# A state-space mixer on one core: SiLU halves joined, and the last quarter's input products moved to ScalarE

## The chip, the cores and the metric

The kernel runs on one core of a Trainium2 chip. The metric is device time in microseconds (us) for the whole program, which computes four layers in one launch. The engines are named as in the profile: PE (TensorE, with PEld for its weight loads), DVE (VectorE), ACT (ScalarE), POOL (GpSimd) and SP (SyncE).

## The reference, cut to what matters

The change lies in layer 0, in the state-space mixer that follows graph attention. Per batch there are 128 nodes, 32 time steps, 256 inner channels and 16 states:

```python
xz = xt @ in_proj
xc, z = xz[..., :D_INNER], xz[..., D_INNER:]
...
xc = silu(xconv)                      # causal convolution over 4 steps
dbc = xc @ x_proj
dt = softplus(dbc[..., :DT_RANK] @ dt_w + dt_b)
Bm, Cm = ...
dA = exp(dt[..., None] * A)
dBx = (dt * xc)[..., None] * Bm[:, :, None, :]
def step(hprev, inp):
    hnew = dA_t * hprev + dBx_t
    y_t = einsum('bds,bs->bd', hnew, C_t)
...
y = (ys + Dp * xc) * silu(z)
return y @ out_w + out_b
```

So each step multiplies the state by a decay, adds an input `u * B` with `u = dt * xc`, and reads the state out with `C`.

## The kernel before, in words

All of layer 0 works on the four batches one after the other. For each, `gat` computes attention, and `mamba` the state-space mixer. The state `S` lies in SBUF as 128 nodes by 16 states by 256 channels.

In `mamba` the 32 steps are cut into 8 blocks of four steps. Per block there is preparation: `mamba_block` makes the convolution (`conv`, four products per half of the channels, L889), its SiLU (`xsilu`, L896), the projections, `dt` and `u`, and the columns `B` and `C` (the tile `BC`); `mamba_gates` makes the gates (`gatep`, L852, and `zsilu`, L859). Both SiLUs work on two halves of 128x512. The first block's `mamba_block` is planned inside the attention stage, all others one block ahead inside `mamba`.

Each step works in four quarters `q` of four states each. For a quarter:

- `decay` (POOL, L667) multiplies `dt` with the rates, into `e`, a tile with three buffers
- `expo` (ACT, L673) takes the exponential into `pa`, a PSUM tile with two buffers
- `mul` (DVE, L687) multiplies `pa` by the state
- `plus` (DVE, L695) adds the input. It issues four instructions, one for each state, each of which computes `u * B + pa`, with `B` as a scale per partition. In the first step of a batch there is nothing to decay, and `plus` only makes the product (L697)
- `diag_pool` (POOL, L684, first two quarters) or `diag` (ACT, L679, last two) makes diagonal matrices of `C`
- `read` (PE, L710) multiplies them with the state and sums over the states, in the PSUM tile `yp`

After the four quarters, `fetch` (ACT, L718) copies the sum out into `y` (two buffers), `turn` (PE, L723 and L728) transposes it into a PSUM bank, and `gate` (DVE, L736) multiplies it by the SiLU of the gates. A block ends with a projection (PE, L773 to L779), a copy (ACT, L785), and a normalization on DVE, POOL and ACT.

The banks of the PSUM tag `pm`, of which there are two, are shared by `turn`, the convolution, the gates and every projection.

The order of the instructions is not written by hand. Each piece of work is a part with an engine, an estimated cost, the parts it comes after, and the buffers that it takes and frees (`hold`). The class `Parts` simulates the engines and picks, part by part, the one that can start first; among those of the same engine that can start within a short patience it takes the one of lowest rank. The rank is the step number times `pace`, plus an offset for the kind of part from the table `RANKS`. The order so found on PE, DVE, ACT and POOL is then kept in the program. Parts whose function differs in its table (`exp`, `ln`, `silu`) make ACT load a table; the load stands in the profile as ACT_TABLE_LOAD at the line of the instruction that needs it.

Of the kernel before, what the change touches and what calls it, by code (L numbers as in the profile page):

```python
# [12 lines left out]
F32 = mybir.dt.float32  # L13
# [110 lines left out]
class Parts:  # L124
# [12 lines left out]
    def hold(self, name, limit):  # L137
        self.limits[name] = limit
        return {"name": name, "free": []}
# [48 lines left out]
class Kernel:  # L188
# [393 lines left out]
    def mamba_weights(self, c, k):  # L582
# [43 lines left out]
        return (inp, xp, dtw, ow, cb, DD, I2, ob4, ntg, ntb, Ar, Wm), built  # L626

    RANKS = dict(
        back=-267, bc=-139.5, bct=18.5, conv=139.5, dabs=-39.5, dbc=10, decay=155.5, dexp=-267, diag=215.5,
        diagp=-284, dln=-315.5, dplus=-240, dsub=-168.5, dtproj=-353, expo=-4, fetch=-214, gate=-583,  # L630
        gatep=361.5, mul=112.5, norm=506.5, ofetch=-562.5, one=-558, plus=-359, power=155.5, project=146,
        read=547.5, relu=-197, shift=-23, stats=284.5, sums=33.5, turn=-293, umul=-243.5, x=667, xproj=-666,
        xsilu=235, xturn=-318, zsilu=203,
    )

    def mamba(self, b, h1, S, blk, gw, mw, m0, w0, m, w, pa, py, pm):
# [6 lines left out]
        inp, xp, dtw, ow, cb, DD, I2, ob4, ntg, ntb, Ar, Wm = mw  # L643
        PE, DVE, ACT, POOL = "PE", "DVE", "ACT", "POOL"
        plan = Parts(window=300, patience=0.15)
        hold, pace = plan.hold, 25.0

        def add(kind, at, *args, **kwargs):
            plan.rank = at * pace + self.RANKS[kind]
            return plan.add(*args, **kwargs)  # L650
# [6 lines left out]
        def step(t, g, before):  # L657

            k, i = divmod(t, 4)
            cs, h, v, parts = slice(i * P, i * P + P), g["h"], {}, {}  # L660

            def node(name):
                return g[name][:, i // 2, i % 2 * 256 : i % 2 * 256 + 256]

            def decay(q):
                v["e", q] = w.tile([P, 4, 256], F32, tag="e", name="e", bufs=3)
                nc.gpsimd.tensor_tensor(  # L667
                    v["e", q], node("dt").unsqueeze(1).to_broadcast([P, 4, 256]), Ar[:, 4 * q : 4 * q + 4, :], ALU.mult
                )

            def expo(q):
                v["a", q] = pa.tile([P, 4, 256], F32, tag="pa", name="pa")
                nc.scalar.activation(v["a", q], v.pop(("e", q)), AF.Exp, scale=-1.0)  # L673

            def diag(q):
                v["D", q] = w.tile([P, 4, 64], F32, tag="D", name="D", bufs=4)
                for r in range(4):
                    s = 16 + 4 * q + r
                    nc.scalar.activation(v["D", q][:, r, :], I2, AF.Copy, scale=g["BC"][:, i, s : s + 1])  # L679

            def diag_pool(q):
                v["D", q] = w.tile([P, 4, 64], F32, tag="Dp", name="Dp", bufs=4)
                C = g["BC"][:, i, 16 + 4 * q : 20 + 4 * q].unsqueeze(2).to_broadcast([P, 4, 64])
                nc.gpsimd.tensor_tensor(v["D", q], I2.unsqueeze(1).to_broadcast([P, 4, 64]), C, ALU.mult)  # L684

            def mul(q):
                nc.vector.tensor_tensor(v["a", q], v["a", q], S[:, 4 * q : 4 * q + 4, :], ALU.mult)  # L687

            def plus(q):
                a = v.pop(("a", q), None)  # L690
                for r in range(4):
                    s = 4 * q + r
                    Bt = g["BC"][:, i, s : s + 1]
                    if t:
                        nc.vector.scalar_tensor_tensor(S[:, s, :], node("u"), Bt, a[:, r, :], ALU.mult, ALU.add)  # L695
                    else:
                        nc.vector.tensor_scalar(S[:, s, :], node("u"), Bt, None, ALU.mult)  # L697

            def read(q):
                if q == 0:
                    v["y"] = py.tile([P, 2, 512], F32, tag="yp", name="yp")
                D = v.pop(("D", q))
                for r in range(4):
                    s = 4 * q + r
                    for n in range(2):
                        o = 64 * ((n + s) % 2)
                        ns = slice(64 * n, 64 * n + 64)
                        nc.tensor.matmul(  # L710
                            v["y"][o : o + 64, n, :256], D[ns, r, :], S[ns, s, :], start=(s < 2), stop=(s >= 14),
                            skip_group_check=True,
                        )

            def fetch():
                y = v.pop("y")
                v["y"] = w.tile([P, 2, 256], F32, tag="y", name="y")
                nc.scalar.copy(v["y"], y[:, :, :256])  # L718

            def turn():  # L720
                v["p"] = bank()
                for j in range(2):
                    nc.tensor.matmul(  # L723
                        v["p"][:, j * P : (j + 1) * P], DD[:, j, :], g["xc"][:, j, cs], start=True, stop=False
                    )
                    for n in range(2):
                        o = j * P + 64 * n
                        nc.tensor.matmul(  # L728
                            v["p"][:, o : o + 64], v["y"][:, n, j * P : (j + 1) * P], I2, start=False, stop=(n == 1)
                        )  # L730

            def gate():
                if i == 0:
                    g["yg"] = m.tile([P, 2, 4, P], F32, tag="yg", name="yg")
                p = v.pop("p")[:, :256].rearrange("p (j n) -> p j n", j=2)
                nc.vector.tensor_tensor(g["yg"][:, :, i, :], p, g["sz"][:, :, cs], ALU.mult)  # L736

            hy, hv = hold("y", 1), hold("yv", 2)
            last = []
            for q in range(4):  # L740
                p = None
                hD = hold("Dp" if q < 2 else "D", 4)
                if t:
                    he, ha = hold("e", 3), hold("pa", 2)
                    p = add("decay", t + q / 4, POOL, 2.36, lambda q=q: decay(q), [g["dt ready"]], [he], [h["dt"]])
                    p = add("expo", t + q / 4, ACT, 1.03, lambda q=q: expo(q), [p], [ha], [he], "exp")
                    p = add("mul", t + q / 4, DVE, 1.23, lambda q=q: mul(q), [p, before["plus", q]])
                if q < 2:
                    d = add("diagp", t + q / 4, POOL, 0.7, lambda q=q: diag_pool(q), [g["BC ready"]], [hD])
                else:  # L750
                    d = add("diag", t + q / 4, ACT, 1.0, lambda q=q: diag(q), [g["BC ready"]], [hD])
                p = parts["plus", q] = add(
                    "plus", t + q / 4, DVE, 1.8, lambda q=q: plus(q),
                    [p, g["u ready"][i // 2], before and before["read", q]],
                    free=[ha, h["u"]] if t else [h["u"]],
                )
                last = [parts.setdefault(("read", q), add(
                    "read", t + q / 4, PE, 1.0, lambda q=q: read(q), [p, d, *last], [] if q else [hy], [hD]
                ))]
            p = add("fetch", t + 1, ACT, 0.6, fetch, last, [hv], [hy])  # L760
            hp = hold("pm", 2)
            p = add("turn", t + 1, PE, 1.5, turn, [p], [hp] if i else [h["yg"], hp], [hv, h["xc"]])
            p = add("gate", t + 1, DVE, 0.45, gate, [p, *g["sz ready"]], (), [hp, h["sz"], h["BC"]])
            g.setdefault("gates", []).append(p)
            return parts
# [78 lines left out]
    def mamba_gates(self, g, k, add, hold, h1, mw, w, pm):  # L844
# [11 lines left out]
        def zsilu(j):  # L856
            if j == 0:
                g["sz"] = w.tile([P, 2, 512], F32, tag="sz", name="sz")
            nc.scalar.activation(g["sz"][:, j, :], g.pop(("z", j)), AF.Silu)  # L859

        zs, first = [], None
        for j in range(2):
            hp = hold("pm", 2)
            first = c = add("gatep", 4 * k, PE, 0.97, lambda j=j: gatep(j), [first], [hp] if j else [h["sz"], hp])
            zs.append(add("zsilu", 4 * k, ACT, 0.6, lambda j=j: zsilu(j), [c, *zs], (), [hp], "silu"))
        g["sz ready"] = zs

    def mamba_block(self, k, add, hold, h1, mw, m, w, pm, after=()):

# [98 lines left out]
            nc.vector.tensor_copy(g["BC"].rearrange("p a b -> p (a b)"), g.pop("bc")[:, :128])  # L968


        xs, first = [], None
        for j in range(2):
            hp = hold("pm", 2)
            first = c = add("conv", 4 * k, PE, 1.95, lambda j=j: conv(j, 0), [first, *after], [hp] if j else [h["xc"], hp])
            c = add("conv", 4 * k, PE, 1.95, lambda j=j: conv(j, 2), [c])
            xs.append(add("xsilu", 4 * k, ACT, 0.7, lambda j=j: xsilu(j), [c, *xs], (), [hp], "silu"))
        hp, hb, h1_ = hold("pm", 2), hold("dbc", 1), hold("u1", 1)
        c = add("xproj", 4 * k, PE, 1.95, xproj, xs, [hb, hp])
        c = add("dbc", 4 * k, ACT, 0.65, dbc, [c], (), [hp])
# [2035 lines left out]
```

## Time and profile before

| what | us |
|---|---|
| median of three runs | 3962.16 (3951.46 to 3969.95) |
| profiled execution, own time | 3967.12 |
| span of the profiled execution | 3965.3 |
| DVE busy in the span | 3090.5 (78%) |
| PE busy | 3227.2 (81%) |
| ACT busy | 2609.6 (66%) |
| POOL busy | 2400.4 (61%) |
| from first to last decay, four batches | 415.9, 415.6, 411.7, 415.6 |

The shares are means over the whole program. The four stretches in which decays run (1659 us together) are what the change touches, besides the first block's parts in the attention stages between them; layers 1 to 3, from about 2400 us on, have none of its code. The lines of the profile give, for a group of instructions, the line of the kernel, engine, operation, tiles written and read, shapes and count, and then busy time, the mean duration of one in ns, and the idle time of the engine ahead of them with what ended it. Groups whose instructions overlap have a busy time below count times duration.

### The profile page before, as it was taken

How to read it: one execution, taken by the hardware profiler on the slowest of the kernel's cores; microseconds unless marked ns; L12 is line 12 of the kernel's file. 1: busy time of each engine (PE TensorE's matmuls, PEld its weight loads, DVE VectorE, ACT ScalarE, POOL GpSimd, SP SyncE). 2: the span in 40 equal slices, each digit the busy share in tenths (PEclk: the TensorE clock that was granted, in tenths of full speed). 3: DMA queues.
4: the chain of work that ended last, by engine and by line, in shares of the span. 5: the costliest groups of instructions: out<-in, count | busy, mean ns of one | idle time of the engine just before them, and what ended most of it. 6: DMA issues, size and time to landing. Idle time of an engine off the chain costs nothing. (4 is left out here: it accounts for less than half of the span.)

```text
span 3965.3 us, 64167 instructions
## 1 busy us (share of the span) xinstructions
PE 3227.2 (81%) x23297; PEld 2075.9 (52%) x23297; DVE 3090.5 (78%) x7595; ACT 2609.6 (66%) x5093; POOL 2400.4 (61%) x1786
## 2 busy tenths in 40 slices
PE   6888887888888888878888869787847787988877
PEld 3445544444544454544444548655535663587655
DVE  6799997799997799997899975668757866286952
ACT  5799875798864798865899853334544556166763
POOL 2599883699873699973799860233444443066940
PEclk8999889999888999998999885888769998998999
DMA  3000000000000000000000000000020000600003
GB/s 122 1 1 1 1 1 1 1 1 1 1 1 1 1 1 1 1 1 1 1 1 1 1 17 2 1 1 1 1 87 8 1 1 1 256 7 1 1 1 86
DMA packets 51548, 61.34 MB, mean 15 GB/s; under 512 B 5743, under 2 KB 31036, under 8 KB 51100
## 3 DMA queue, kind: packets, MB, share of 16 engines
q1 hardware_dynamic: 36636, 42.12, 3.1%
q10 hardware_dynamic: 14592, 15.08, 1.1%
q8 instruction: 187, 3.06, 0.3%
q14 instruction: 133, 1.09, 0.1%
HBM read 48.79 MB, written 8.39 MB: 14 GB/s over the span
## 5 line engine op out<-in xcount | busy, mean ns | idle before, releaser
L667 POOL TENSOR_TENSOR e<-dt,Ar 128x1024 f32<-128x1024 f32 x496 | 1160.9, 2362 | 103.4 <-ACT pa L673 101.0
L695 DVE SCALAR_TENSOR_TENSOR S<-u,BC,pa 128x256 f32<-128x256 f32 x1984 | 820.8, 476 | 28.4 <-PE yp L710 0.5
L687 DVE TENSOR_TENSOR pa<-pa,S 128x1024 f32<-128x1024 f32 x496 | 607.3, 1224 | 49.3 <-ACT pa L673 49.0
L673 ACT ACTIVATE pa<-e 128x1024 f32<-128x1024 f32 x496 | 504.8, 1023 | 126.8 <-DVE S L695 114.4
L710 PE MATMUL yp<-S,D 64*64 64x256 f32 x4096 | 378.4, 414 | 101.7 <-DVE S L695 87.3
L710 PE MATMUL yp<-S,Dp 64*64 64x256 f32 x4096 | 342.9, 452 | 51.2 <-DVE S L695 38.4
L710 PEld LDWEIGHTS yp<-S,D 64*64 64x64 f32 x4096 | 186.4, 140 | 264.4 <-DVE S L695 153.8
L465 POOL TENSOR_TENSOR e<-e,den 128x512 f32<-128x512 f32 x128 | 132.2, 1043 | 257.2 <-DVE den L461 193.2
L710 PEld LDWEIGHTS yp<-S,Dp 64*64 64x64 f32 x4096 | 175.7, 153 | 203.5 <-issue 118.1
L679 ACT ACTIVATE D<-I,BC 128x64 f32<-128x64 f32 x1024 | 260.7, 334 | 0.6 <-PE yp L710 0.6
L889 PE MATMUL pm<-h,Wm 128*128 128x512 f32 x512 | 240.1, 604 | 1.2 <-ACT h L525 1.2
L728 PE MATMUL pm<-I,y 128*128 128x64 f32 x1024 | 165.1, 289 | 89.7 <-ACT y L718 89.7
L453 ACT ACTIVATE e<-sc,mn 128x128 f32<-128x128 f32 x512 | 143.9, 391 | 98.1 <-DVE mn L448 96.6
L728 PEld LDWEIGHTS pm<-I,y 128*128 128x128 f32 x1024 | 152.4, 214 | 101.9 <-ACT y L718 101.9
L673 ACT ACT_TABLE_LOAD x144 | 184.8, 1283 | 19.4 <-DVE S L695 17.2
L684 POOL TENSOR_TENSOR Dp<-I,BC 128x256 f32<-128x256 f32 x256 | 164.4, 660 | 20.1 <-PE yp L710 10.4
L251 POOL TENSOR_TENSOR rs<-rs,mhalf 128x4 f32<-128x4 f32 (+1 forms) x33 | 38.6, 1171 | 220.0 <-DVE rs L250 181.7
L448 DVE TENSOR_REDUCE mn<-sc 128x4 f32<-128x512 f32 x128 | 83.4, 685 | 87.8 <-PE sc L440 55.9
L889 PEld LDWEIGHTS pm<-h,Wm 128*128 128x128 f32 x512 | 90.9, 191 | 92.3 <-issue 90.2
L723 PE MATMUL pm<-xc,DD 128*128 128x128 f32 x512 | 127.8, 334 | 5.3 <-ACT sz L859 4.6
L723 PEld LDWEIGHTS pm<-xc,DD 128*128 128x128 f32 x512 | 87.6, 210 | 64.9 <-issue 38.0
L2607 ACT ACTIVATE xn<-X,xnb,xrs 128x128 f32<-128x128 f32 x192 | 80.7, 488 | 42.6 <-DMA lnw<-in_L_attn_ln_w_dram 30.3
(587 smaller groups left out, 8025.7 us busy)
## 6 DMA issues: line engine op xcount, KB each, us to landing
w<-in_L_ffn_weight_dram SPq DMA_DIRECT2D x22, 1024.0 KB
w<-in_L_ffn_weight_dram ACTq DMA_DIRECT2D x10, 1024.0 KB
out_dram<-o ACTq DMA_DIRECT2D x16, 256.0 KB
out_dram<-o SPq DMA_DIRECT2D x16, 256.0 KB
X<-in_x_dram SPq DMA_DIRECT2D x4, 512.0 KB
A<-in_L_conv_A_log_dram SPq DMA_DIRECT2D x1, 2048.0 KB
cw<-in_L_conv_conv_w_dram SPq DMA_DIRECT2D x1, 512.0 KB
sh<-in_sh_dram SPq DMA_DIRECT2D x1, 512.0 KB
```

What stands on the lines that cost most here:

```text
L453: nc.scalar.activation(e[:, i, :], v["sc"][:, h, i * P : (i + 1) * P], AF.Exp, scale=-1.0, bias=v["mn"][:, 4 * h + i : 4 * h + i + 1],)
L465: nc.gpsimd.tensor_tensor(v["e", h], v["e", h], den, ALU.mult)
L667: nc.gpsimd.tensor_tensor(v["e", q], node("dt").unsqueeze(1).to_broadcast([P, 4, 256]), Ar[:, 4 * q : 4 * q + 4, :], ALU.mult)
L673: nc.scalar.activation(v["a", q], v.pop(("e", q)), AF.Exp, scale=-1.0)
L679: nc.scalar.activation(v["D", q][:, r, :], I2, AF.Copy, scale=g["BC"][:, i, s : s + 1])
L684: nc.gpsimd.tensor_tensor(v["D", q], I2.unsqueeze(1).to_broadcast([P, 4, 64]), C, ALU.mult)
L687: nc.vector.tensor_tensor(v["a", q], v["a", q], S[:, 4 * q : 4 * q + 4, :], ALU.mult)
L695: nc.vector.scalar_tensor_tensor(S[:, s, :], node("u"), Bt, a[:, r, :], ALU.mult, ALU.add)
L710: nc.tensor.matmul(v["y"][o : o + 64, n, :256], D[ns, r, :], S[ns, s, :], start=(s < 2), stop=(s >= 14), skip_group_check=True,)
L723: nc.tensor.matmul(v["p"][:, j * P : (j + 1) * P], DD[:, j, :], g["xc"][:, j, cs], start=True, stop=False)
L728: nc.tensor.matmul(v["p"][:, o : o + 64], v["y"][:, n, j * P : (j + 1) * P], I2, start=False, stop=(n == 1))
L889: nc.tensor.matmul(g["x", j], Wm[:, i, j * P : (j + 1) * P], rows(4 * k + 3 - i), start=(i == 0), stop=(i == 3))
```

## The change

It has four parts. First, both halves of the gates' SiLU become one part for the planner, `both`, which issues the two instructions next to each other; it takes both banks of `pm` with the first product and frees both after the second SiLU. Second, the same for the convolution's SiLU, in all blocks but the first of each batch, whose halves stay parts of their own. Third, in the last quarter of every step but the first of a batch, four instructions of ACT compute `u * B` into a new SBUF tile `ub` (one buffer), and `plus_all` adds it to the decayed state with one 128x1024 instruction of DVE in place of four 128x256 ones. Fourth, the table of ranks is replaced, `pace` goes from 25.0 to 25.5, and the planner's cost for the remaining `plus` goes from 1.8 to 1.85.

```diff
-        back=-267, bc=-139.5, bct=18.5, conv=139.5, dabs=-39.5, dbc=10, decay=155.5, dexp=-267, diag=215.5,
-        diagp=-284, dln=-315.5, dplus=-240, dsub=-168.5, dtproj=-353, expo=-4, fetch=-214, gate=-583,
-        gatep=361.5, mul=112.5, norm=506.5, ofetch=-562.5, one=-558, plus=-359, power=155.5, project=146,
-        read=547.5, relu=-197, shift=-23, stats=284.5, sums=33.5, turn=-293, umul=-243.5, x=667, xproj=-666,
-        xsilu=235, xturn=-318, zsilu=203,
+        back=-71.5, bc=24.5, bct=-76, conv=596, dabs=234.5, dbc=-130.5, decay=82.5, dexp=-227.5, diag=299,
+        diagp=-572.5, dln=-701.5, dplus=-237.5, dsub=21, dtproj=-847.5, expo=-47, fetch=-40.5, gate=-880.5,
+        gatep=612, mul=323.5, norm=669, ofetch=-424.5, one=-518.5, plus=-486, power=-93, project=64, read=678,
+        relu=-237, shift=358, stats=955.5, sums=96, turn=-70, ub=68.5, umul=-351.5, x=687, xproj=-282.5,
+        xsilu=69.5, xturn=-201.5, zsilu=278,
...
-        hold, pace = plan.hold, 25.0
+        hold, pace = plan.hold, 25.5
...
+            def inputs(q):
+                v["b", q] = w.tile([P, 4, 256], F32, tag="ub", name="ub", bufs=1)
+                for r in range(4):
+                    s = 4 * q + r
+                    nc.scalar.activation(v["b", q][:, r, :], node("u"), AF.Copy, scale=g["BC"][:, i, s : s + 1])
+
+            def plus_all(q):
+                S4 = S[:, 4 * q : 4 * q + 4, :]
+                nc.vector.tensor_tensor(S4, v.pop(("a", q)), v.pop(("b", q)), ALU.add)
...
+                far = q == 3 and t
+                if far:
+                    hb = hold("ub", 1)
+                    b = add("ub", t + q / 4, ACT, 1.76, lambda q=q: inputs(q), [g["u ready"][i // 2], g["BC ready"]], [hb], [h["u"]])
                 p = parts["plus", q] = add(
-                    "plus", t + q / 4, DVE, 1.8, lambda q=q: plus(q),
-                    [p, g["u ready"][i // 2], before and before["read", q]],
-                    free=[ha, h["u"]] if t else [h["u"]],
+                    "plus", t + q / 4, DVE, 1.23 if far else 1.85, lambda q=q, f=plus_all if far else plus: f(q),
+                    [p, b if far else g["u ready"][i // 2], before and before["read", q]],
+                    free=[ha, hb] if far else [ha, h["u"]] if t else [h["u"]],
                 )
...
-        zs, first = [], None
+        hs, c = [hold("pm", 2), hold("pm", 2)], None
         for j in range(2):
-            hp = hold("pm", 2)
-            first = c = add("gatep", 4 * k, PE, 0.97, lambda j=j: gatep(j), [first], [hp] if j else [h["sz"], hp])
-            zs.append(add("zsilu", 4 * k, ACT, 0.6, lambda j=j: zsilu(j), [c, *zs], (), [hp], "silu"))
-        g["sz ready"] = zs
+            c = add("gatep", 4 * k, PE, 0.97, lambda j=j: gatep(j), [c], () if j else [h["sz"], *hs])
+
+        def both():
+            zsilu(0)
+            zsilu(1)
+
+        g["sz ready"] = [add("zsilu", 4 * k, ACT, 1.2, both, [c], (), hs, "silu")]
...
-        xs, first = [], None
+        hs, xs, c, first = [hold("pm", 2), hold("pm", 2)], [], None, None
         for j in range(2):
-            hp = hold("pm", 2)
-            first = c = add("conv", 4 * k, PE, 1.95, lambda j=j: conv(j, 0), [first, *after], [hp] if j else [h["xc"], hp])
+            take = [hs[j]] if after else [] if j else hs
+            c = add("conv", 4 * k, PE, 1.95, lambda j=j: conv(j, 0), [first if after else c, *after], take if j else [h["xc"], *take])
+            first = first or c
             c = add("conv", 4 * k, PE, 1.95, lambda j=j: conv(j, 2), [c])
-            xs.append(add("xsilu", 4 * k, ACT, 0.7, lambda j=j: xsilu(j), [c, *xs], (), [hp], "silu"))
+            if after:
+                xs.append(add("xsilu", 4 * k, ACT, 0.7, lambda j=j: xsilu(j), [c, *xs], (), [hs[j]], "silu"))
+
+        def both():
+            xsilu(0)
+            xsilu(1)
+
+        xs = xs or [add("xsilu", 4 * k, ACT, 1.4, both, [c], (), hs, "silu")]
```

## The prediction

> **What bounds the kernel now.** I first read the groups of instructions of the whole execution, to see what the state-space stage consists of. In each row the numbers after the bar are busy time, mean duration of one in ns, and idle time of the engine just before.
>
> ```profile
> L667 POOL TENSOR_TENSOR e<-dt,Ar 128x1024 f32<-128x1024 f32 x496 | 1160.9, 2362 | 103.4 <-ACT pa L673 101.0
> L695 DVE SCALAR_TENSOR_TENSOR S<-u,BC,pa 128x256 f32<-128x256 f32 x1984 | 820.8, 476 | 28.4 <-PE yp L710 0.5
> L687 DVE TENSOR_TENSOR pa<-pa,S 128x1024 f32<-128x1024 f32 x496 | 607.3, 1224 | 49.3 <-ACT pa L673 49.0
> ...
> L679 ACT ACTIVATE D<-I,BC 128x64 f32<-128x64 f32 x1024 | 260.7, 334 | 0.6 <-PE yp L710 0.6
> ...
> L673 ACT ACT_TABLE_LOAD x144 | 184.8, 1283 | 19.4 <-DVE S L695 17.2
> ...
> L859 ACT ACT_TABLE_LOAD x64 | 82.1, 1283 | 1.1
> ...
> L896 ACT ACT_TABLE_LOAD x60 | 77.0, 1283 | 1.1
> ```
>
> There are 496 quarters of a step (31 steps x 4 quarters x 4 batches; a batch's first step has no decay). Each is a chain over three engines: decay (POOL), exp (ACT), multiply and four additions (DVE). Four additions overlap: 820.8 / 496 = 1.655 us a quarter, not 4 x 0.476. L859 and L896 are SiLU: 64 of 64 and 60 of 64 halves load a table, and the exp at L673 loads its own table back.
>
> The decays of L667 fall into four stretches, one per batch. The table of stretches, cut at them (time, then busy time of PE, weight loads, DVE, ACT, POOL), gives each engine's load there:
>
> ```profile
> 171.40:587.30 415.90, 353.87 (x2830) 205.73 (x2829) 389.26 (x729) 362.62 (x582) 384.62 (x222) 0.91 0.00 1
> 755.00:1170.60 415.60, 354.09 (x2829) 206.05 (x2827) 389.20 (x728) 362.72 (x582) 384.51 (x223) 0.91 0.00 1
> 1342.10:1753.80 411.70, 348.66 (x2827) 201.60 (x2825) 388.48 (x728) 362.09 (x582) 384.74 (x223) 0.93 0.00 1
> 1922.20:2337.80 415.60, 352.23 (x2828) 204.43 (x2827) 389.51 (x728) 362.69 (x582) 384.49 (x223) 0.91 0.00 1
> ```
>
> A stage lasts 414.7 us on average. DVE works 389.1 of it (25.6 idle), POOL 384.6 (30.1), ACT 362.5 (52.2). DVE is fullest, POOL is only 4.5 us behind. Then the waits of the first stage (total us, times, longest):
>
> ```profile
> POOL e L667 <- ACT pa L673: 26.4, 18, 3.2
> ...
> ACT pa L673 <- DVE S L695: 25.1, 24, 2.1
> ...
> DVE pa L687 <- ACT pa L673: 11.9, 9, 5.7
> ACT xn L785 <- PE pm L779: 11.2, 7, 2.0
> ```
>
> Read them upwards from DVE: ACT waits until DVE's additions free one of the two exp buffers in PSUM (25.1), and because ACT is late POOL waits for one of its three decay buffers (26.4). DVE itself waits 11.9 for exp. So DVE sets the pace through the buffers, and relief for DVE is felt by all three, until POOL's own 384.6 stops it.
>
> **The change part by part.** *Last quarter on DVE.* 31 quarters a stage lose four additions (1.655 us) and get one 128x1024 addition of a PSUM and an SBUF operand. The nearest row is L687, same engine, size and kinds of operand: 1.224. It can hardly be less; with a slow SBUF write I allow 1.3. Gain 0.431 x 31 = 13.4 us a stage (11.0 at 1.3). DVE: 389.1 - 13.4 = 375.7.
>
> *Last quarter on ACT.* Four products u x B, 128x256, with a scale per partition. No row has this form at this length. L679 is the same operation at 64 elements: 334 ns alone, 260.7 / 1024 = 255 in a row. From L718 (128x512, 579) and L673 (128x1024, 1023) an element costs 0.867 ns, so 256 elements take 334 + 192 x 0.867 = 500 alone, 421 in a row: 3 x 421 + 500 = 1.76 us. The Trainium skill, "ScalarE: Activation LUTs" ("What ACT_TABLE_LOAD costs"), has 280 ns + 0.833 per element and 93 overlap, an estimate of 1.69. I take 1.70, ends 1.6 and 1.8: x 31 = +52.7 (49.6 to 55.8). The same page's rules for kernel authors speak against the move: multiplications belong on VectorE. The trace agrees on price: L697 does this product on DVE for a batch's first step, 64 in 17.4 us, so 1.09 a quarter against 1.70. By that rule the quarter would cost DVE 1.09 + 1.22 = 2.31, or stay at 1.655. I go against the rule because DVE has 25.6 us idle a stage and ACT 52.2.
>
> *SiLU halves joined.* A stage has 8 gate blocks and 7 convolution blocks (the eighth lies in the attention stage, and its halves stay apart). Each joined pair loses one SiLU load and one load back. In the first stage I count 36 + 16 + 13 + 7 = 72 loads; after, 8 + 7 SiLU, 7 ln and 22 returns, 44. Saved: 28. Their price, from ACT's instructions in order of time:
>
> ```profile
> 315.22 1.28 ACT L859 ACT_TABLE_LOAD   x1
> 316.51 0.60 ACT L859 ACTIVATE sz<-pm 128x512 f32<-128x512 f32 x1
> 317.13 1.28 ACT L673 ACT_TABLE_LOAD   x1
> 318.42 1.03 ACT L673 ACTIVATE pa<-e 128x1024 f32<-128x1024 f32 x1
> ```
>
> SiLU ends at 317.11, the load starts at 317.13 and the exp follows 0.01 us after it. The Trainium skill, same section, adds about 1.38 us of drain to each load, 2.66 a switch. By it 28 switches would be 74.5 us a stage; by the trace they are 28 x 1.283 = 35.9, and the trace shows no room for a drain. I take 35.9. ACT: 362.5 + 52.7 - 35.9 = 379.3.
>
> *Waits and holds.* The wide addition waits for the products too. Behind it on DVE stand the next step's multiplies and the gate; PE's last reads of the step wait for it. The products need only u and B, made a block ahead, and the single ub buffer, free since the last step's addition; ACT has some 10 us to place them. Cost 0, covered by ACT's idle time; uncovered, each us of lateness at all 124 places is 124 us. PE may read the quarter 1.22 us after the addition starts rather than from 0.48 to 1.66: between 0.4 earlier and 0.7 later, taken as 0. The joined parts take both PSUM banks of tag pm at once; taken as 0 here, and it is the rival below. *Ranks and pace* reorder ready parts on every engine, the first block's parts inside attention too. They add no instruction; no row prices them. DVE's present waits are some 15 us a stage, which bounds a gain; a loss of the same size bounds the other side, and I take 0. No DMA moves; SP and its queue are untouched.
>
> *Sum for a stage.* Before: DVE 389.1, POOL 384.6, ACT 362.5. After: POOL 384.6, ACT 379.3, DVE 375.7. If the fullest engine keeps the old idle time, a stage takes 384.6 + 25.6 = 410.2 (-4.5). If only DVE's work counts, it takes 414.7 - 13.4 = 401.3 (-13.4). POOL then has 16.7 idle, below its present 30.1 but possible, as 26.4 of that is the echo of DVE. ACT would have 22.0, of which 11.2 is already its wait for PE's projection. With three engines within 9 us of each other I take 407, nearer to the first: -7.7 a stage, -31 in four. The next thing late is POOL.
>
> The profiled execution took 3967.1 us (span 3965.3 and 1.8 around it), 4.9 above the median of the runs, 3962.2. The difference is carried over: 3962 - 31 = 3931.
>
> **The rivals.** *No change (22%).* ACT's new work takes the slack that let DVE run. Before, 52 us of idle ACT absorbed the SiLU detours; now ACT has under 36. If DVE's waits for exp rise from 11.9 by the 13.4 saved, the stage stays at 414.7: 3962. For it: ACT, POOL and DVE come within 9 us. Against: a pair of detours of 3.2 us becomes one of 3.9, and exps already wait for DVE 24 times a stage.
>
> *Slower (26%): the two banks.* PE's convolution of a block takes 7.5 us (16 products, 604 ns less overlap) and ACT's load and two SiLUs 2.7, so both banks are held for 10.2 us at best. In the trace the same work, from the first product of a block (326.9) to its last SiLU (342.6), is spread over 15.7, with a projection in the other bank between. A step is 414.7 / 32 = 13.0 us; its turn needs a bank, and with two yv buffers it can be about one step late before the next fetch, the reads and DVE stand. A hold of 15.7 costs 2.7 a block, x 28 = 76, less the gain of 31: +45, 4007. It decides once the stall passes 31 / 28 = 1.1 us a block, a hold of 14.1. Against: the order on PE is written with the hold known.
>
> *The freer end (part of the 52% for the first case).* If the stage falls to 401.3, four give -54: 3908; with a better order it could reach 398, 3895.
>
> **How the numbers follow.** Faster 52%, at 3931. A measurement of this kernel tells some 0.5% (20 us) from no change. Faster by more than that: 0.52; within: 0.22; slower: 0.26. The likeliest case's own range is 3895 to 3942. The range, 3892 to 3996, adds no change, the milder half of the bank case and up to 9 us a stage of unlucky order, and leaves out the worst banks and the luckiest order.
>
> **What would show it.** Right: L859 and L896 loads near 32 and 36, L673's returns near 88 to 96, DVE 375 to 378 a stage, ACT 376 to 383, POOL still 384.6 and now fullest, stages near 407, POOL's wait for exp under 26. Products near 1.7 a quarter, the wide addition at 1.22. Wrong: long waits of DVE for ACT's products or exps (no change), or of PE for a pm bank held by SiLU, with the gate late (slower). I am wrong at the root if stages shrink while DVE's busy time doesn't, or if the time moves in attention.

## The result, and the profile after

The changed kernel takes 3917.95 us (median of four runs, 3915.67 to 3921.49) against 3966.05 for the kernel before on the same chip: ratio 0.9879, 95% interval 0.9861 to 0.9898. That is 48 us less; 31 were forecast. The profiled execution has a span of 3917.3 (before 3965.3).

The groups of the whole execution that answer to those shown before the prediction:

```profile
L703 ACT ACTIVATE ub<-u,BC 128x256 f32<-128x256 f32 x496 | 210.6, 498 | 0.6 <-DVE S L707 0.3
...
L707 DVE TENSOR_TENSOR S<-pa,ub 128x1024 f32<-128x1024 f32 x124 | 151.7, 1224 | 5.8
...
L673 ACT ACT_TABLE_LOAD x88 | 112.9, 1283 | 1.6
...
L915 ACT ACT_TABLE_LOAD x36 | 46.2, 1283 | 0.6
L956 ACT ACT_TABLE_LOAD x32 | 41.1, 1283 | 0.6
L874 ACT ACT_TABLE_LOAD x32 | 41.1, 1283 | 0.6
```

The new products cost 210.6 / 124 = 1.70 us a quarter, the wide addition 1.224. The SiLU of the gates (now L874) loads its table 32 times instead of 64, that of the convolution (L915) 36 instead of 60, and the exp loads back 88 times instead of 144.

The table of stretches from first to last decay of each batch (time, then busy time of PE, weight loads, DVE, ACT, POOL, and then the clock granted to PE as a share of full speed):

```profile
168.90:571.20 402.30, 341.19 (x2812) 199.50 (x2804) 376.37 (x641) 369.94 (x685) 384.21 (x223) 0.91 0.00 1
739.10:1143.30 404.20, 343.72 (x2814) 200.75 (x2806) 376.75 (x641) 370.51 (x685) 384.17 (x222) 0.90 0.00 1
1309.80:1711.00 401.20, 338.00 (x2829) 197.16 (x2822) 376.52 (x641) 371.41 (x687) 384.20 (x222) 0.92 0.00 1
1879.30:2286.30 407.00, 348.89 (x2821) 205.44 (x2814) 376.70 (x641) 370.46 (x685) 384.46 (x222) 0.88 0.00 1
```

A stage takes 403.7 us instead of 414.7. Four times 11.0 make 44 of the 48 us; the attention stages between, the start and the end make the other 4 (-4.9, -2.5 and +3.5). POOL's work is what it was, 384.3, and it is now the fullest engine; its idle time fell from 30.1 to 19.4. DVE is at 376.6, ACT at 370.6. The waits of the first stage (total us, times, longest):

```profile
...
ACT y L728 <- PE yp L720: 17.6, 6, 3.7
...
POOL e L667 <- ACT pa L673: 14.2, 12, 3.7
...
DVE pa L687 <- ACT pa L673: 11.2, 15, 5.6
```

POOL's wait for ACT fell from 26.4 to 14.2. ACT's long wait for DVE to free an exp buffer (25.1 before) is gone from the top of the list: in the stage's groups it is 6.3 (4.9 on L695, 1.4 on L707).

### The profile page after: what moved, and what is told of

Read it like the earlier page. It is cut to its first block, busy times and chain, and to the rows that moved or that the text cites. A ratio compares the mean times of both kernels' runs of the same rounds, so it can differ in the third digit from the quotient of the medians.

```text
span 3917.3 us, 64096 instructions
## 1 busy us (share of the span) xinstructions
PE 3186.5 (81%) x23297; PEld 2062.7 (53%) x23297; DVE 3034.0 (77%) x7223; ACT 2637.5 (67%) x5477; POOL 2397.4 (61%) x1786
## 5 line engine op out<-in xcount | busy, mean ns | idle before, releaser
L687 DVE TENSOR_TENSOR pa<-pa,S 128x1024 f32<-128x1024 f32 x496 | 607.8, 1225 | 53.2 <-ACT pa L673 52.4
L695 DVE SCALAR_TENSOR_TENSOR S<-u,BC,pa 128x256 f32<-128x256 f32 x1488 | 615.2, 475 | 20.0
L720 PE MATMUL yp<-S,Dp 64*64 64x256 f32 x4096 | 352.1, 469 | 91.1 <-DVE S L695 47.4
L720 PE MATMUL yp<-S,D 64*64 64x256 f32 x4096 | 320.4, 417 | 59.5 <-DVE S L707 29.8
L720 PEld LDWEIGHTS yp<-S,Dp 64*64 64x64 f32 x4096 | 185.2, 160 | 237.5 <-issue 137.9
L720 PEld LDWEIGHTS yp<-S,D 64*64 64x64 f32 x4096 | 162.0, 142 | 202.8 <-ACT D L679 58.6
L703 ACT ACTIVATE ub<-u,BC 128x256 f32<-128x256 f32 x496 | 210.6, 498 | 0.6 <-DVE S L707 0.3
L707 DVE TENSOR_TENSOR S<-pa,ub 128x1024 f32<-128x1024 f32 x124 | 151.7, 1224 | 5.8
L728 ACT COPY y<-yp 128x512 f32<-128x512 f32 x128 | 73.8, 577 | 98.7 <-PE yp L720 98.6
```

Source lines behind the costliest of these rows:

```text
L703: nc.scalar.activation(v["b", q][:, r, :], node("u"), AF.Copy, scale=g["BC"][:, i, s : s + 1])
L707: nc.vector.tensor_tensor(S4, v.pop(("a", q)), v.pop(("b", q)), ALU.add)
L720: nc.tensor.matmul(v["y"][o : o + 64, n, :256], D[ns, r, :], S[ns, s, :], start=(s < 2), stop=(s >= 14), skip_group_check=True,)
```

## The experiments

All ratios are to the kernel before on the same chip. Its medians on the chips used lie within 1 us of each other (3965.4 to 3966.3), so times from different chips are also compared directly. The first four versions are planned anew with the parts they have; all others keep the changed kernel's order of parts and only emit something else in its place. Figures "a stage" are means of the four stretches, and a profile line shown is that of the first.

**Ranks alone**, on the structure of before (`RANKS`, `pace` and the planner's 1.85 from the diff, nothing else).

> The kernel before with the new ranks, pace and planner cost alone; no joined halves, no moved products. Theory (VectorE's relief is paid for by ScalarE's saved table loads): the busy times stay at 389 us DVE, 384.6 POOL and 362.5 ACT a stage, so the time stays within 20 us of before, 3946 to 3986. Rival (the new order is what gained): at or below 3936, at least 30 of the 48 us.

Measured: 4063.2 us, ratio 1.0258 (1.0217 to 1.0298), 98 us slower. Both are wrong. The work is the same, and a stage takes 441.4 (439.7 the first):

```profile
169.40:609.10 439.70, 364.23 (x2830) 210.53 (x2824) 387.38 (x731) 362.14 (x586) 384.60 (x222) 0.88 0.00 1
```

DVE's 387.7, ACT's 362.2 and POOL's 384.6 are within 2 us of those of before. So 27 us a stage (441.4 - 414.7) can be lost to the order alone. A table of ranks that serves one set of parts can be bad for another.

**Joined halves alone**, with the new ranks (the diff's parts in `mamba_gates` and `mamba_block`).

> Only the SiLU halves are joined, with the new ranks; the last quarter stays four additions on DVE. Theory: ACT falls by some 36 us a stage to about 327, DVE stays at 389 and bounds the stage: 0 to 5 us less a stage, 3946 to 3966. Rival (the detours of ACT for its tables were what held the chain up): most of the gain is here, 3936 or less.

Measured: 3966.8, ratio 1.0006 (0.9989 to 1.0023). As the theory said, ACT is at 326.6 a stage, DVE at 386.9, and nothing is gained on before (the time is 1 us above the theory's range):

```profile
172.40:587.80 415.40, 360.07 (x2821) 207.81 (x2815) 385.04 (x727) 326.59 (x558) 384.02 (x223) 0.90 0.00 1
```

Against ranks_only, which shares the ranks but not the order found with them, the joins are worth 96 us.

**Last quarter alone**, with the new ranks, and **with the old ones**:

```diff
-        bc=..., umul=-243.5,
+        bc=..., umul=-243.5, ub=300,      # quarter_old_ranks only
...
+                b = add("ub", t + q / 4, ACT, 1.76, lambda q=q: inputs(q), ...)
```

> Only the last quarter's products go to ScalarE and the wide addition to DVE, with the new ranks; the SiLU halves stay apart. Theory: DVE falls to 376 a stage, but ACT rises to 362.5 + 49 = some 412 of work with its table loads kept, so ACT bounds the stage at 420 to 430: slower than before, 3985 to 4030. Rival (DVE's work alone sets the stage): some 404 a stage as in the changed kernel, near 3920.

> The same as quarter_only but with the ranks and pace of before, and a rank of 300 for the products. It tells whether the order chosen for the new ranks matters for that half of the change. Theory: ACT is the bound by its work, so again slower than before, 3985 to 4040, and within 20 us of quarter_only. Rival (the order decides): it lies more than 30 us from quarter_only.

Measured: 4111.0, ratio 1.0361 (1.0323 to 1.0398), and 4238.3, ratio 1.0686 (1.0650 to 1.0722). Both are slower, and by more than the theory's numbers. In quarter_only ACT is the fullest engine:

```profile
166.70:625.30 458.60, 372.76 (x2820) 217.19 (x2812) 383.63 (x653) 414.23 (x722) 388.91 (x227) 0.84 0.00 1
```

ACT has 414 us of work, but the stage is 459, so ACT is 44 idle as well. The two differ by 127 us, so the second rival, that the order decides, holds for the size. In both versions the SiLU halves are apart, as before.

**The loads brought back**, in the changed kernel's order:

```diff
         def both():
             zsilu(0)
+            nc.scalar.activation(w.tile([P, 1], F32, tag="scr", name="scr"), self.ones[:, 0:1], AF.Exp)
             zsilu(1)
```

(the same for `xsilu`).

> The changed kernel in its own order, but between the two joined SiLUs stands a one-column exponential into a scratch tile, so that ACT loads its tables again as often as before: 28 to 30 more loads a stage, 15 small exponentials. ACT rises from 370.6 by 30 x 1.283 + 15 x 0.28 = 43 to some 413. Theory (the loads saved pay for the products): ACT becomes the bound, a stage at 420 to 440 against 403.7, so 3985 to 4065. Rival (ACT has slack that hides it): below 3950.

Measured: 4067.3, ratio 1.0253 (1.0230 to 1.0277). ACT works 414.1 a stage, as forecast (a small exponential took 203 ns, where 0.28 us was taken), and the stage is 442.7, a little over the theory's range for it. DVE waits 37.4 us a stage for exp (13.1 in the changed kernel) and 13.2 in front of the gate (3.4). ACT is idle for 28.6 of the 442.7, so its work alone does not fill the stage here either.

**The quarter given back to DVE**, in the same order:

```diff
-                    b = add("ub", t + q / 4, ACT, 1.76, lambda q=q: inputs(q), ...
+                    b = add("ub", t + q / 4, ACT, 1.76, lambda: None, ...
...
-                    ... lambda q=q, f=plus_all if far else plus: f(q),
+                    ... lambda q=q, f=plus: f(q),
```

> The changed kernel in its own order, with the last quarter as four additions of DVE again and no products on ACT: DVE 376.6 + 13.4 = 390 a stage, ACT 370.6 - 51 = 320. Theory (DVE's work sets the pace): a stage takes 11 to 16 us more, 3962 to 3982, although ACT has far less to do. Rival (the gain is in the order or in the loads): within 15 us of the changed kernel, 3903 to 3933.

Measured: 3934.2, ratio 0.9921 (0.9905 to 0.9938). This stands against my theory: a third of the gain goes, not all of it. The time lies 1 us above the rival's range. The profiled execution was the fastest of the four (3920.7, the others 3932 to 3939), so it does not show where the 16 us of the medians go:

```profile
169.30:573.70 404.40, 352.26 (x2813) 203.85 (x2805) 381.25 (x727) 324.17 (x563) 384.10 (x223) 0.91 0.00 1
```

DVE is at 381.7 on average, not 390; 5.0 us of the difference are told under the hardware below. POOL waits here as little as in the changed kernel (17.6 us a stage against 17.7).

**Neither half, in the same order**: both edits together.

> In the changed kernel's own order, both halves of the change are taken back: four additions of DVE in the last quarter and no products on ACT, and a one-column exponential between the two joined SiLUs that brings the loads back. Work of ACT a stage: 324.8 + 43 = some 368, as before (362.5), DVE 382 to 389. Theory (the saved loads are what the 32 us between before and quarter_back are): 3955 to 3985. Rival (the order alone made them): 3924 to 3944.

Measured: 4052.8, ratio 1.0218 (1.0201 to 1.0235). Both expectations are wrong: taken back in this way, the kernel is 87 us slower than before. This does not price the order alone. The loads stand between two SiLUs that hold both banks meanwhile, which no kernel with the halves apart does, and the small exponentials are extra work. With the three others it makes a table, in one order (us):

| | quarter on DVE | quarter on ACT and DVE |
|---|---|---|
| a table load between the halves | 4052.8 | 4067.3 |
| halves joined | 3934.2 | 3918.0 |

The quarter is worth 16 us with the joins and costs 15 without them. The missing loads between the halves are worth 119 to 149 in this order. Planned anew each time, the joins were worth 96 (ranks_only to joins_only) and 193 (quarter_only to the changed kernel).

**Four narrow additions** of the same products:

```diff
-                S4 = S[:, 4 * q : 4 * q + 4, :]
-                nc.vector.tensor_tensor(S4, v.pop(("a", q)), v.pop(("b", q)), ALU.add)
+                a, b = v.pop(("a", q)), v.pop(("b", q))
+                for r in range(4):
+                    nc.vector.tensor_tensor(S[:, 4 * q + r, :], a[:, r, :], b[:, r, :], ALU.add)
```

> The changed kernel in its own order, with ScalarE's products, but added by four 128x256 additions instead of one of 128x1024. It tells whether DVE gains by losing the multiplication or by losing three instructions. Theory: the multiplication was free in the fused instruction, so four plain additions take some 1.6 us as before, DVE is back at some 388 and the time at 3955 to 3975. Rival: a plain addition of 256 is cheaper than the fused one, and the time stays within 15 us of 3918.

Measured: 3930.2, ratio 0.9904 (0.9887 to 0.9920). The rival is right. DVE's group:

```profile
L708 DVE TENSOR_TENSOR S<-pa,ub 128x256 f32<-128x256 f32 x496 | 175.6, 416 | 5.8
```

Four narrow additions take 175.6 / 124 = 1.42 us a quarter, between the fused 1.655 and the wide 1.224. Of the 0.43 us saved, 0.24 come from dropping the multiplication and 0.19 from the width. The multiplication in the fused instruction is not free: 476 ns alone with it, 416 without.

**Less work for POOL**: the addition of the norm's shift `ntb` is left out, and the output lacks it.

> The changed kernel in its own order, with one of the three POOL operations of a block's end left out (the addition of the last norm's shift, so the output lacks it): POOL loses 8 x 1.28 = 10.2 us a stage, 384.3 to some 374. It tells what bounds the changed kernel. Theory (POOL is now next): a stage loses 4 to 8 us, 3886 to 3902. Rival (DVE still sets the pace, or ACT): under 2 us a stage, 3910 to 3920.

Measured: 3854.3, ratio 0.9722 (0.9705 to 0.9739), 64 us below the changed kernel. The gain is at least twice the forecast: POOL lost 7.7 us a stage in the stretch, the stage 13.7 (403.7 to 390.0), and DVE's busy time fell by 8.1 though none of its work was touched. So POOL's work matters, but this run does not show that it alone bounds. That led to the next three.

**The norm's epsilon by ACT** in place of DVE's 128x4 operation, and the same **with less work for POOL**, and **with some matrices of `C` by ACT** in place of POOL:

```diff
...
-                nc.vector.tensor_scalar(g["rs"], g["mv"][:, :, 1], 1e-5, None, ALU.add)
...
             def power():
+                nc.scalar.activation(g["rs"], g["mv"][:, :, 1], AF.Identity, bias=self.eps5)
                 nc.gpsimd.tensor_tensor(g["rs"], g["rs"], self.mhalf.to_broadcast([P, 4]), ALU.pow)
...
             def diag_pool(q):                      # eps_act_diag only
+                if q == 1 and i == 3:
+                    for r in range(4):
+                        s = 16 + 4 * q + r
+                        nc.scalar.activation(v["D", q][:, r, :], I2, AF.Copy, scale=g["BC"][:, i, s : s + 1])
+                    return
```

> The changed kernel in its own order, with the 128x4 addition of the norm's epsilon (2.1 us each on DVE, while POOL works) made by ACT instead. DVE falls by 12.6 us a stage to 364. Theory (POOL bounds the changed kernel): 1 to 4 us a stage, 3902 to 3914. Rival (DVE's work still sets the pace): 8 us a stage or more, below 3888.

> eps_act with the addition of the last norm's shift on POOL left out too (the output lacks it): POOL 10.2 us a stage less, with DVE's slow 128x4 operation out of the way. Theory (POOL bounds): 8 to 10 us a stage below eps_act, 32 to 40 us in all. Rival (in pool_less it was DVE's shorter waits for POOL that counted): under 5 us a stage below eps_act.

> eps_act, and the diagonal matrices of the second quarter are made by ACT instead of POOL in every fourth step: POOL 8 x 0.62 = 5 us a stage less, ACT 8 x 1.05 = 8.4 more. Theory (POOL bounds, ACT has some 30 us idle): 3 to 5 us a stage below eps_act, 12 to 20 us in all, some 3890. Rival (ACT, in a fixed order, is too full): no faster than eps_act.

Measured: 3891.8, ratio 0.9801 (0.9776 to 0.9825); 3859.7, ratio 0.9740 (0.9724 to 0.9757); 3909.8, ratio 0.9857 (0.9841 to 0.9874). eps_act lies between the two expectations; it is the fastest of the versions that compute the whole reference, 74 us below before. Taking POOL's addition away from it gives another 32 us, 8.9 a stage (398.0 to 389.1), as the theory had it. But DVE fell by 7.6 there too, and without POOL's addition the epsilon's move gains nothing (3859.7 against 3854.3 in pool_less). Moving matrices to ACT does not help, and the rival is right: POOL falls by 4.4 to 379.5 a stage, ACT rises by 7.1 to 378.2, the stage stays at 398.8, and the time is 18 us above eps_act.

## Why the prediction was right, and where not

**DVE's part: right.** The wide addition took its neighbour's 1.224 us; DVE came out at 376.6 a stage, 375.7 forecast.

**ACT's products: price right.** Four took 1.70 us as taken, 498 ns for one alone, where the rows had given 500 and the Trainium skill, "ScalarE: Activation LUTs" ("What ACT_TABLE_LOAD costs"), gives an estimate of 493.

**Loads: count and price right.** The three lines shown had 268 loads and now have 156: 112 fewer, 28 for each batch, at 1283 ns each. With a drain of 1.38 us for each, as the same page has it, 28 fewer would have freed another 39 us of ACT a stage (an estimate); the instructions stand back to back in both profiles. Alone, the joins took 35.6 us off ACT's work (362.2 in ranks_only, 326.6 in joins_only), and 35.9 were forecast.

**ACT's sum: 8.7 us too high, in the products.** It came to 370.6 instead of 379.3. In one order the products add 45.8 us a stage (324.8 in quarter_back to 370.6), not 52.7, and with the loads brought back 45.7 (368.5 in neither_same_order to 414.1). ACT's instructions in order of time show the reason:

```profile
322.39 0.58 ACT L728 COPY y<-yp 128x512 f32<-128x512 f32 x1
322.87 1.70 ACT L703 ACTIVATE ub<-u,BC 128x256 f32<-128x256 f32 x4
324.48 1.01 ACT L673 ACTIVATE pa<-e 128x1024 f32<-128x1024 f32 x1
...
338.66 1.03 ACT L673 ACTIVATE pa<-e 128x1024 f32<-128x1024 f32 x1 [0.48 <-POOL e L667]
339.71 1.28 ACT L915 ACT_TABLE_LOAD   x1
341.00 1.27 ACT L915 ACTIVATE xc<-pm,conv_b 128x512 f32<-128x512 f32 x2
```

The four products start 0.10 us before the copy ahead of them ends, and the next exp starts 0.09 us before they end. The sum counted the overlap among the four, but not that with their neighbours: 1.70 - 0.19 = 1.51 us, near the 45.8 / 31 = 1.48 measured. A load overlaps neither neighbour, so its whole price is saved with it.

**The waits and banks: right.** DVE never waited for the products (L707 has no releaser in its idle time, 5.8 us in all). Its wait in front of the gate fell from 4.0 to 3.4 us a stage, and PE's waits for SiLU from 4.3 to 3.0, so the bank rival did not happen. Whether its mechanism is at work elsewhere is not shown. The wait in front of the gate is 13.2 in loads_back and 14.3 in neither_same_order, where loads stand inside the hold; but it is 11.0 in ranks_only and 13.0 in quarter_only too, where no part holds both banks.

**What is fullest next: right. That it bounds: in part.** POOL is fullest, at 384.3. Leaving out its addition moved the stage most (13.7 and 8.9 us). But taking 4.4 us from it by way of ACT moved nothing, and eps_act lost 5.7 us a stage with POOL's work unchanged.

**The term that was mis-sized: the order, taken as 0 with bounds of 15 us a stage.** With the work of before, the new ranks cost 27 us a stage. (The 15 were DVE's waits for ACT and POOL in the first stage; with those for PE they are 21.6.) With the work of the joined halves alone, the order's price can be read by itself: joins_only and quarter_back have the same instructions (7595 on DVE, 4981 on ACT, 1786 on POOL) and differ only in their order. They take 3966.8 and 3934.2 us, a difference of 33. So what each half of the change is worth depends on the order in which one looks (us):

| | without the quarter on ACT | with it | the quarter gains |
|---|---|---|---|
| planned anew, halves apart | 4063.2 | 4111.0 | -48 |
| planned anew, halves joined | 3966.8 | 3918.0 | 49 |
| the changed kernel's order, halves joined | 3934.2 | 3918.0 | 16 |

Planned anew, the sum's account holds: the joins alone gain nothing on before, the quarter alone is not paid for, and the two together give the 48 us. In the changed kernel's order only 16 of the 48 go when the quarter is given back; the other 32 stay with the joined halves in an order that was planned with the quarter in view. That is near the lower end of my sum (-4.5 a stage, 18 in all) for DVE's relief by itself. The number forecast, 31 us less, came near in part by luck: the term put at 0 moved the same work by 98 and by 33 us, where the whole gain is 48.

**A reading that was wrong: POOL's wait as an echo of DVE.** In quarter_back the waits of the first stage are:

```profile
ACT pa L673 <- DVE S L695: 39.1, 33, 1.9
...
POOL e L667 <- ACT pa L673: 15.8, 14, 2.3
```

Over the four stages ACT waits 38.3 us for DVE's additions there against 5.3 in the changed kernel (25.2 before), and POOL 15.3 for ACT against 14.2 (25.3 before). So ACT can be kept waiting by DVE without POOL feeling it.

**The rival "no change"** would have shown in longer waits of DVE for exp. They stayed as they were, 12.2 us a stage before and 13.1 after. They rose where the loads are kept: to 34.9 in quarter_only and 37.4 in loads_back, both slower.

**What stays open.** Why one order of the same work is 33 us faster than another: no wait was singled out. Whether other ranks would let the joined halves alone gain something; with the old ranks they were not run. Nor is it shown why eps_act is 26 us faster though DVE's busy time did not fall (377.5); its four stages are uneven, 407.8, 401.3, 391.1 and 391.6. The clock granted to PE goes with the length of a stage (401.2 us at 0.92 and 407.0 at 0.88 in the changed kernel), and which of the two leads was not tested. It did not make the gain, for its mean over the four stages is lower after (0.90) than before (0.92).

## What to carry to other kernels

When three engines are within a few per cent of each other, do not count on more than the distance to the next when work is taken off the fullest, and ask who pays: here ACT's saved table loads, two for each pair of halves, without which the move loses. A hand-made or planned order belongs to one set of instructions: judge an edit and its order together. Putting the old work back into the new order tells what each edit is worth there, and planning each version anew can tell something else (16 and 49 us here): do both before giving credit. A rebalancing that pays with one edit can cost without it (16 us gained, 15 lost).

## What the runs showed of the hardware

A tiny DVE instruction can last as long as what is left of POOL's current one. In the changed kernel the norm's epsilon is added to 128x4 elements. DVE's instructions in order of time, and POOL's:

```profile
344.65 2.10 DVE L810 TENSOR_SCALAR mrs<-mmv 128x4 f32<-128x4 f32 x1
346.66 1.22 DVE L687 TENSOR_TENSOR pa<-pa,S 128x1024 f32<-128x1024 f32 x1
```

```profile
344.37 2.35 POOL L667 TENSOR_TENSOR e<-dt,Ar 128x1024 f32<-128x1024 f32 x1
346.83 1.02 POOL L813 TENSOR_TENSOR mrs<-mrs,mhalf 128x4 f32<-128x4 f32 x1
```

It starts 0.28 us after a decay and ends when the decay does, 346.75 against 346.72. The profile counts this as DVE's busy time. Over all 32 it lasts from 169 to 2221 ns. The 24 that start while a decay runs all end within 0.03 us of its end; the other 8 start with POOL idle and take 170 ns. The Trainium skill, "GPSIMD Engine Reference" ("Specifications"), says that POOL shares its SBUF interface with DVE instructions that run in a two-port mode or read two SBUF inputs, and the rows fit: this one, from SBUF to SBUF, and the 128x4 instruction `mnb` after it, with two SBUF inputs, are slow, and those with one input in PSUM (L687, L695) are not. To go from SBUF to SBUF is not enough by itself, though: the norm's BATCH_NORM_STATS2 and BATCH_NORM_AGGREGATE do so too, at 277 and 150 ns (median). In which mode L810 runs, no row shows. With epsilon moved to ACT, the wait only went to `mnb`, 498 ns on average in the changed kernel's stages and 2869 in eps_act's:

```profile
L819 DVE SCALAR_TENSOR_TENSOR mnb<-mmv,mrs x32: 143/2308/6929, 242.8 to 2277.0; 128x4 f32<-128x4 f32 x32
```

The three numbers are the least, median and longest duration in ns. The longest, 6929, starts at 294.20 us and ends with the third of three decays in a row (294.13 to 301.10), so it can wait for more than one POOL instruction. The two instructions together, count times mean in the four stretches, took 16.3 us a stage before, 15.6 in the changed kernel, 10.6 in quarter_back and 8.9 in pool_less. How much of a POOL instruction they meet thus changes with the order and also, at one order, with the timing (changed kernel and pool_less). DVE's busy time in quarter_back is 7.4 us a stage below that of before, and 5.7 of it are this time. What this time does to the length of a stage was not isolated.
